# Four graph-attention layers on sixteen graphs: adjacency of two graphs cast on the way into SBUF, weight preparation in the scheduled list, rank tables for the first and last graphs

## The chip, the cores and the metric

The kernel runs on one core of a Trainium2 chip. A core has TensorE (PE, matrix products), VectorE (DVE), ScalarE (ACT), GpSimd (POOL) and SyncE (SP, which issues transfers), each with its own queue of instructions, executed in order. The metric is the device time of one execution in microseconds (us). A measurement of this kernel is the median of several executions.

## The reference

There are B = 16 graphs with N = 1024 nodes and D = 128 features. The input `adj` is [16, 1024, 1024] in int32, each entry 0 or 1, with ones on the diagonal and about one entry in 256 set besides. Four attention layers follow one another, each added to its input and normalised:

```python
x = _layernorm(x + _L0_gnn_ref(x, adj, ...), axis=-1)   # scores by edge type, types 0 and 1 here
x = _layernorm(x + _L1_gnn_ref(x, adj, ...), axis=-1)   # one head, masked by adj > 0
x = _layernorm(x + _L2_gnn_ref(x, adj, ...), axis=-1)   # graph norm, 8 heads, elu, graph norm, 1 head, elu
x = _layernorm(x + _L3_gnn_ref(x, adj, ...), axis=-1)   # one head, masked by adj
```

Layer 0 takes, for each pair of nodes, the score that belongs to its edge type (`take_along_axis` over `src . a_t . dst`), a leaky ReLU, a softmax over all neighbours and a product with the values. Layers 1 and 3 are single-head graph attention: `softmax(where(adj, leaky(s1_i + s2_j), -inf)) @ (x W)`. Layer 2 has an eight-head and a single-head attention of this kind, each behind a normalisation over the graph.

## The kernel before

Nodes are laid out as 128 partitions times G = 8. All data of a graph stay in SBUF from layer to layer. What the attention steps read of the adjacency is `maskT`, the transposed adjacency as fp8 [128, 8, 1024], one per graph, of which four places exist.

**How the order comes about.** `graph(b)` does not issue instructions; it records them. `rc.vector`, `rc.tensor` and the like go to a `Recorder`, which notes each operation, what it depends on and a modelled cost (`cost_of`). `rc.either` notes an operation that two engines can do (a copy, an affine step, the comparison in `products`), and the planner chooses. After all sixteen graphs are recorded, `rc.run(rank, window, later)` plays through the list with the modelled costs: at each step it takes the operation that can start earliest, and among those with equal start the one with the lowest rank. The result is one fixed order for each engine, which `issue` writes out. So nearly all instructions carry one line in the profile, L412, the line in `issue`, and are told apart by the names of their tiles.

The rank of an operation is `graph * STEP + position in its graph + SHIFT[...] + ENDS[graph]`. `SHIFT` has 40 entries over a graph's length, `ENDS` one entry per graph. `later` adds a bias for each engine and kind where an operation may go to two engines. `AHEAD = 3` lets four graphs be open at a time. Tiles come from shelves with a fixed number of places: 28 of `row` (128 x 1032 f32), 8 PSUM banks `bank`, 4 `maskT`, 3 `half`, 2 each of the DRAM scratch `adj` and `up`; a tile's place comes free when its last reader has run. The model prices a cast transfer on POOL at 4 us and 100 bytes per ns.

**Where the mask comes from.** For graph 0 (`b < DIRECT`, `DIRECT = 1`), SyncE loads eight blocks of 128 rows as int32; ScalarE casts each to bf16 and sums it (`e_sum`), TensorE transposes it in eight 128 x 128 pieces, and ScalarE copies the turned block to `maskT` as a square with a second sum (`e_sq`). The two sums, equal when all entries are 0 or 1, are compared at the end. For every other graph, POOL casts the whole adjacency to bf16 in DRAM (`scratch`, profile name `adj`), SyncE issues eight transposing transfers into `half` and eight stores to `upright` (profile name `up`), and POOL brings it back as fp8 into `maskT`. Four ScalarE passes over `maskT` (`half<-maskT`) write a count into `edges`, which is checked at the end. The first cast waits for `begun[0]`, a copy on POOL behind the transposed input `hT` of graph 0.

**Weights.** Some 60 operations ahead of the recorded list, issued directly and therefore first on every queue, load all weights and derive `kwT`, `vpT`, `cbias`, `fold`, `fold_b` (layer 0), `w1_v` (layer 1), `w2a_e`, `w2b_v`, `gn1`, `gn2`, `same_group` (layer 2) and `w3_v` (layer 3). `a_types` is the type tensor of layer 0 turned from [e, t] to [t, e] on POOL. The input of graph 0 is the first load of all, into the place `vs`.

**Layer by layer, per graph.** Layer 0: `transpose_nodes`, three projections, then for two halves of the nodes eight blocks: two products of width 512, `copy_predicated` on `maskT`, a ReLU on ScalarE, a sum with maximum on VectorE, then exponentials and the product with the values. Layers 1, 2b and 3 use `projected_head`: a projection with two score columns, `factors` (a store `a_d` and a load back, broadcast to all partitions), eight masked rows by `weights_of` and 64 products. Layer 2's eight heads use `products`: comparisons on ScalarE or VectorE, a bitwise and with `maskT`, fp8 by bf16 products, and `combine`. The last step is the store to `out` on SyncE. After all graphs a short check over the collected ranges decides whether a general path is run.

Of the kernel before, what the change touches and what calls it, by code (L numbers as in the profile page):

```python
# [109 lines left out]
class Op:  # L110
    __slots__ = ("ways", "way", "skip", "graph", "rank", "before", "after", "ready", "slots", "missing", "late", "kind")


class Recorder:
# [5 lines left out]
    CAST_RATE = 100.0  # L120

    def __init__(self, nc, tc):
        self.nc, self.tc, self.ops, self.graph = nc, tc, [], 0
        self.access = {}

# [36 lines left out]
    def cost_of(self, engine, name, args, kw, outs, ins):  # L162
# [19 lines left out]
        if engine == "gpsimd":  # L182
            if name == "dma_start":
                size = mybir.dt.size(aps[1].dtype) * aps[0].shape[0] * self.width(o)
                return 1500.0, 4000.0 + size / self.CAST_RATE
            return 200.0 + 2.0 * n, 100.0
# [32 lines left out]
    def either(self, *ways, skip=None, kind=0):  # L219
# [6 lines left out]
        op.rank = at = len(self.ops)  # L226
        touched = []
# [37 lines left out]
    def run(self, rank, window, later):  # L265
# [60 lines left out]
        moved = 0.0  # L326

        def admit(i):
            for way in ops[i].ways:
                pools[way[0]].append((i, way, ranks[i] + (later[way[0]][ops[i].kind] if len(ops[i].ways) > 1 else 0)))  # L330
# [25 lines left out]
        while len(order) < n:  # L356
# [41 lines left out]
            if way[0] == "sync":  # L398
                moved = max(moved, end) + way[5]
                op.late = moved - end + self.DMA_FIXED  # L400
            finish(i, end, op.late)
# [22 lines left out]
def gnn_stack_kernel(ctx: ExitStack, tc: tile.TileContext, w: dict, out: bass.AP):  # L424
# [11 lines left out]
    def fast_path(stack):  # L436
# [31 lines left out]
        class Scratch:  # L468


            def __init__(self, *flats):
                self.free, self.named = [(f, 0) for f in flats], {}

            def tile(self, shape, dt, tag, name):
                n = 1
                for v in shape[1:]:
                    n *= v
                if tag not in self.named:
                    k = next(k for k, (f, at) in enumerate(self.free) if at + n <= f.shape[1])
                    f, at = self.free[k]  # L480
                    self.free[k], self.named[tag] = (f, at + n), f[:, at : at + n]
                flat = self.named[tag][0 : shape[0], 0:n]
                if len(shape) > 2:
                    flat = flat.rearrange("p (a b) -> p a b", a=shape[1])
                return flat

        ppool = Scratch(shelves["m4"].places[0], shelves["x4"].places[0])
        turns = [0]

        def ps_const(*shape):  # L490
            turns[0] += 1
            flat = shelves["bank"].places[4 + turns[0] % 4]
            n = 1
            for v in shape:
                n *= v
            return flat[:, 0:n]

        first_x = shelves["vs"].places[0][:, 0 : G * (D + 1)].rearrange("p (g f) -> p g f", g=G)
        nc.sync.dma_start(out=first_x[:, :, 0:D], in_=x_in[0].rearrange("(p g) f -> p g f", g=G))


# [9 lines left out]
        def load(ap, name, shape=(P, D), pool=None):  # L511
            t = (pool or cpool).tile(list(shape), F32, tag=name, name=name)
            nc.sync.dma_start(out=t, in_=ap)
            return t

        def load_rows(vec, n, name):
            return load(vec.partition_broadcast(P), name, (P, n), ppool)

        def column(vec):
            return vec.rearrange("(p o) -> p o", o=1)  # L520

        def transposed(src, name, pool=None):
            ps = ps_const(P)
            nc.tensor.transpose(ps, src, ident)
            t = (pool or cpool).tile([P, P], F32, tag=name, name=name)
            nc.vector.tensor_copy(t, ps)
            return t


        qw = load(w["L0_gnn_qw"], "qw", pool=ppool)  # L530
        kw = load(w["L0_gnn_kw"], "kw", pool=ppool)
        kwT = transposed(kw, "kwT")
        pw = load(w["L0_gnn_pw"], "pw", pool=ppool)
        pwT = transposed(pw, "pwT", ppool)
        vw = load(w["L0_gnn_vw"], "vw", pool=ppool)
        qb = load(column(w["L0_gnn_qb"]), "qb", (P, 1))
        kb = load(column(w["L0_gnn_kb"]), "kb", (P, 1))
        vb = load(column(w["L0_gnn_vb"]), "vb", (P, 1))
        pb = load_rows(w["L0_gnn_pb"], D, "pb")
        ps = ps_const(D)  # L540
        nc.tensor.matmul(ps, lhsT=vw, rhs=pwT, start=True, stop=True)
        vpT = const([P, D], "vpT")
        nc.vector.tensor_copy(vpT, ps)
        vb_wide = ppool.tile([P, P], F32, tag="vb_wide", name="vb_wide")
        nc.vector.tensor_copy(vb_wide, vb.to_broadcast([P, P]))
        ps = ps_const(D)
        nc.tensor.matmul(ps, lhsT=vb_wide, rhs=pwT, start=True, stop=True)
        cbias = const([P, D], "cbias")
        nc.vector.tensor_add(cbias, ps, pb)
        a_types = ppool.tile([P, T, D], F32, tag="a_types", name="a_types")  # L550
        a_raw = ppool.tile([P, D, T], F32, tag="a_raw", name="a_raw")
        nc.sync.dma_start(out=a_raw, in_=w["L0_gnn_a"])
        nc.gpsimd.tensor_copy(a_types, a_raw.rearrange("p e t -> p t e"))


        fold = const([P, 2, D], "fold")
        fold_b = const([P, 2], "fold_b")
        for t in range(2):
            ps = ps_const(D)
            nc.tensor.matmul(ps, lhsT=qw, rhs=a_types[:, t, :], start=True, stop=True)  # L560
            nc.vector.tensor_scalar(fold[:, t, :], ps, 0.2, None, ALU.mult)
            ps = ps_const(1)
            nc.tensor.matmul(ps, lhsT=a_types[:, t, :], rhs=qb, start=True, stop=True)
            nc.vector.tensor_scalar(fold_b[:, t : t + 1], ps, 0.2, None, ALU.mult)

        def score_vector(wt, a_rows, groups, name):
            k = D // groups
            prod = ppool.tile([P, groups, k], F32, tag="prod", name="prod")
            nc.vector.tensor_tensor(
                prod,  # L570
                wt.rearrange("p (g k) -> p g k", g=groups),
                a_rows.unsqueeze(1).to_broadcast([P, groups, k]),
                ALU.mult,
            )
            v = const([P, groups], name)
            nc.vector.tensor_reduce(v, prod, AX.X, ALU.add)
            return v

        def score_weights(wt, a_src, a_dst, groups, name):
            k = D // groups  # L580
            src = score_vector(wt, load_rows(a_src, k, name + "_as"), groups, name + "_src")
            dst = score_vector(wt, load_rows(a_dst, k, name + "_ad"), groups, name + "_dst")
            return src, dst

        def halves(a):
            flat = a if len(a.shape) == 1 else a.rearrange("k o -> (k o)")
            n = flat.shape[0] // 2
            return flat[0:n], flat[n : 2 * n]

        w1 = load(w["L1_gnn_W"], "w1", pool=ppool)  # L590
        w1_s = score_weights(w1, *halves(w["L1_gnn_a"]), 1, "l1")
        w2a = load(w["L2_gnn_W1"], "w2a", pool=ppool)
        w2a_s = score_weights(w2a, *halves(w["L2_gnn_a1"]), NH, "l2a")
        w2b = load(w["L2_gnn_W2"], "w2b", pool=ppool)
        w2b_s = score_weights(w2b, *halves(w["L2_gnn_a2"]), 1, "l2b")
        w3T = transposed(load(w["L3_gnn_W"], "w3", pool=ppool), "w3T", ppool)
        w3_s = score_weights(w3T, *halves(w["L3_gnn_a"]), 1, "l3")


        gn1 = [load(column(w[f"L2_gnn_gn1_{k}"]), f"gn1_{k}", (P, 1)) for k in ("alpha", "scale", "shift")]  # L600

        NA = P // G
        member = ppool.tile([NA, P], F32, tag="member", name="member")
# [9 lines left out]
        gn2_raw = ppool.tile([NA, 3, NH], F32, tag="gn2_raw", name="gn2_raw")  # L613
        for i, k in enumerate(("alpha", "scale", "shift")):
            nc.sync.dma_start(
                out=gn2_raw[:, i, :], in_=w[f"L2_gnn_gn2_{k}"].rearrange("(h a) -> a h", a=NA)
            )
        ps = ps_const(3 * NH)
        nc.tensor.matmul(
            ps, lhsT=member, rhs=gn2_raw.rearrange("a i h -> a (i h)"), start=True, stop=True  # L620
        )
        gn2 = const([P, 3, NH], "gn2")
        nc.vector.tensor_copy(gn2.rearrange("p i h -> p (i h)"), ps)
        ps = ps_const(P)
        nc.tensor.matmul(ps, lhsT=member, rhs=member, start=True, stop=True)
# [559 lines left out]
        for b in range(B):  # L1185
            rc.graph = b
            graph(b)
# [664 lines left out]
```

## Time and profile before

| | |
|---|---|
| time, median of 3 executions | 2499.18 us (2498.39 to 2500.36) |
| profiled execution, its own time | 2502.76 us |
| its span, first to last instruction | 2500.9 us |
| granted TensorE clock, mean | 0.975 |
| busy: PE / PE weight loads | 2351.2 us (94%) / 1999.5 us (80%) |
| busy: VectorE / ScalarE / POOL | 2267.2 us (91%) / 1807.6 us (72%) / 25.1 us (1%) |
| chain that ended last, by engine | PE 58%, DVE 36%, ACT 3%, issue 2%, DMA 1% |
| cast transfers `adj<-in_adj_dram` | 15, 17.6 us from issue to landing (median) |
| return transfers `maskT<-up` | 15, 8.2 us from issue to landing (median) |

The profile is of one execution, so sums of its rows belong to that execution's time, not to the median. An engine's busy share is an average over the whole span, and the stretches of the span have different limits; times within the span count from its first instruction. In a row of instructions "x" is a count, "mean" the duration of one, and "idle before" the time in which the engine had nothing to do just ahead of them, with what ended that wait. An f32 product appears as two records.

### The profile page before, as it was taken

The numbers are of one execution on the slowest core, as the hardware profiler recorded it, in microseconds if no ns is written. First come the engines' busy times: TensorE is split into PE (matmuls) and PEld (weight loads), VectorE is DVE, ScalarE is ACT, GpSimd is POOL, SyncE is SP. The second block draws the span as 40 slices with busy tenths as digits, with TensorE's granted clock in tenths as the row PEclk, the third lists the DMA queues.
The fourth block names the chain that finished last, engine by engine and source line by source line (L and its number), as shares of the span: only waits on it lengthen the run. The fifth ranks groups of instructions, "written<-read, shape, count | busy, mean of one in ns | idle before, by whom it ended". The sixth has DMA issues, their size and how long they took to land.

```text
span 2500.9 us, 56272 instructions
## 1 busy us (share of the span) xinstructions
PE 2351.2 (94%) x22981; PEld 1999.5 (80%) x22981; DVE 2267.2 (91%) x5079; ACT 1807.6 (72%) x3373; POOL 25.1 (1%) x41
## 2 busy tenths in 40 slices
PE   7889999999999999999999999999999999978975
PEld 4758797978979787897869889797888878777965
DVE  3489899999999999999989999999999989889975
ACT  4388595958779686877949688696867858796922
POOL 0000000000000000000000000000000000000000
PEclk8999999999999999999999999999999999989987
DMA  9772226062441706234052442607152222111100
GB/s 223 144 183 49 77 53 174 13 144 86 92 130 21 192 28 139 91 90 132 19 135 86 96 125 50 180 10 171 59 129 93 65 64 86 33 54 48 57 18 27
DMA packets 227738, 229.31 MB, mean 92 GB/s; under 512 B 135056, under 2 KB 171152, under 8 KB 225552
## 3 DMA queue, kind: packets, MB, share of 16 engines
q1 hardware_dynamic: 209712, 178.45, 25.1%
q0 software_dynamic: 17760, 47.19, 10.2%
q8 instruction: 182, 2.98, 0.5%
q14 instruction: 84, 0.69, 0.1%
HBM read 200.76 MB, written 72.02 MB: 109 GB/s over the span
## 4 chain that ended last, share of the span: by engine, by line
PE 58%; DVE 36%; ACT 3%; issue 2%; DMA 1%; POOL 0%; SPq 0%; ACTq 0%; DVEq 0%
PE bank L412 58%; DVE row L412 25%; DVE x L412 5%; ACT row L412 2%; DVE sums L412 1%; DVE bank L412 1%; DVE mv L412 1%; DVE mf L412 1%; DVE m L412 0%; DVE top_all L412 0%; DVE rdens L412 0%; DVE rs_q L412 0%; DVE rden_h L412 0%; DMA m<-in_L_gnn_a_dram 0%; DVE c L412 0%
## 5 line engine op out<-in xcount | busy, mean ns | idle before, releaser
L412 PE MATMUL bank<-row,row 128*128 128x129 f32 (+1 forms) x9216 | 1438.7, 314 | 33.4 <-DVE row L412 19.5
L412 PEld LDWEIGHTS bank<-row,row 128*128 128x128 f32 x9216 | 1122.0, 193 | 215.4 <-issue 143.9
L412 ACT ACTIVATE row<-row,bs2h 128x1024 fp8e4<-128x1024 f32 x684 | 737.7, 1143 | 13.6 <-PE bank L412 13.5
L412 DVE SCALAR_TENSOR_TENSOR row<-row,ratio,maskT 128x1024 f32<-128x1024 f32 x384 | 466.8, 1277 | 12.5 <-DMA row<-a_d 11.5
L412 PEld LDWEIGHTS <-row 128*128 128x128 fp8e4 x8192 | 402.1, 97 | 39.8 <-issue 19.8
L412 PE MATMUL bank<-m,row 128*128 128x102 bf16 x8192 | 420.4, 208 | 10.6 <-DVE row L412 6.2
L412 DVE TENSOR_TENSOR row<-row,maskT 128x2048 uint16<-128x2048 uint16 x256 | 308.9, 1214 | 0.9 <-ACT row L412 0.7
L412 DVE TENSOR_SCALAR row<-row,ns 128x1024 fp8e4<-128x1024 f32 x340 | 244.6, 743 | 0.0
L412 ACT ACTIVATE row<-bank 128x512 f32<-128x512 f32 x256 | 149.4, 594 | 126.1 <-DVE bank L412 114.0
L412 PEld LDWEIGHTS <-maskT 128*128 128x128 fp8e4 x3072 | 201.0, 97 | 24.2 <-issue 22.2
L412 PE MATMUL bank<-m,maskT 128*128 128x136 bf16 x3072 | 211.3, 225 | 5.1 <-DVE m L412 2.6
L412 DVE COPY_PREDICATED bank<-maskT,bank 128x512 f32<-128x512 uint8 x256 | 175.2, 689 | 24.4 <-PE bank L412 23.0
L412 DVE CUSTOM_DVE_ANT_0 row<-bank,row 128x512 f32<-128x512 f32 x256 | 172.8, 681 | 9.9 <-ACT row L412 9.0
L412 PE MATMUL bank<-ident,row 128*128 128x128 f32 x624 | 115.7, 288 | 32.0 <-ACT row L412 24.0
L412 DVE TENSOR_REDUCE x<-bank 128x136 f32<-128x408 f32 x256 | 142.4, 571 | 2.2 <-PE bank L412 1.8
L412 ACT ACTIVATE row<-row,top_all 128x1024 f32<-128x1024 f32 x128 | 139.8, 1141 | 4.9 <-DVE top_all L412 4.8
L412 ACT ACTIVATE row<-row 128x1024 f32<-128x1024 f32 x32 | 33.8, 1056 | 145.1 <-DVE row L412 138.0
L412 ACT ACTIVATE sq<-row 128x128 f32<-128x128 f32 x256 | 76.5, 300 | 84.9 <-DVE row L412 78.9
L412 PEld LDWEIGHTS bank<-ident,row 128*128 128x128 f32 x624 | 78.0, 145 | 58.0 <-ACT row L412 41.9
L412 ACT ACTIVATE half<-maskT,minus_half 128x2048 fp8e4<-128x2048 fp8e4 x60 | 119.6, 1999 | 0.0
L412 DVE SCALAR_TENSOR_TENSOR row<-bank,rdens,row 128x128 f32<-128x128 f32 x368 | 109.6, 342 | 0.2
L412 ACT ACTIVATE row<-bank,exps 128x128 f32<-128x128 f32 x219 | 67.2, 362 | 30.8 <-DVE row L412 29.3
(233 smaller groups left out, 2200.6 us busy)
## 6 DMA issues: line engine op xcount, KB each, us to landing
row<-s1d SPq DMA_DIRECT2D x128, 512.0 KB
adj<-in_adj_dram POOLq DMA_DIRECT2D x15, 2048.0 KB, 17.6
up<-half SPq DMA_DIRECT2D x120, 256.0 KB
row<-a_d SPq DMA_DIRECT2D x48, 512.0 KB
maskT<-up POOLq DMA_DIRECT2D x15, 1024.0 KB, 8.2
out_dram<-row SPq DMA_DIRECT2D x16, 512.0 KB
row<-in_x_dram SPq DMA_DIRECT2D x15, 512.0 KB
row<-in_adj_dram SPq DMA_DIRECT2D x8, 512.0 KB
```

Source lines behind the costliest of these rows:

```text
L412: done = getattr(getattr(self.nc, engine), name)(*[real(a) for a in args], **{k: real(a) for k, a in kw.items()})
```

## The change

Four things change in `fast_path` and in the `Recorder`.

1. `DIRECT` is 2. For graphs 0 and 1 POOL issues four transfers each that cast a quarter of the adjacency from int32 in DRAM to bf16 in SBUF, into `row` places. TensorE transposes each block as before, and the copy into `maskT` is an operation that ScalarE or VectorE can do. `e_sum` and `e_sq` go; the count into `edges` is now made for graphs 0 and 1 too. These casts wait for `begun[0]`, which is now a copy on POOL behind `types`; the casts of the other graphs to DRAM wait for `begun[1]`, the former signal behind `hT` of graph 0. The loads of `x` for graphs 2 and later wait for it as well.
2. The weight preparation is recorded in the list. Layer 0's weights (`weights_of_layer0`, nine loads) come ahead of graph 0 with rank -2000, behind the load of graph 0's input; of the type tensor only two types are turned, on VectorE. All other weights (`weights_of_the_rest`, eighteen loads) are recorded behind layer 0 of graph 0 and ranked at that position.
3. The planner's price of a cast transfer becomes 1 us of issue, 210 bytes per ns one after another, and 4 us at the end.
4. An operation's position `op.at` is counted per graph, with the extra operations of graphs 0 and 1 held at one position. `STEP`, `SHIFT`, `ENDS` and `LATER` have new values, and there are new tables: `FIRST` (20 entries over a graph's length, added for graphs 0 to 2), `FINAL` (20 entries, added for the last three graphs) and `LAST` (added to the engines' biases for the last three graphs).

The diff, cut to its core:

```diff
-    CAST_RATE = 100.0
+    CAST_RATE, CAST_FIXED = 210.0, 4000.0
...
-                return 1500.0, 4000.0 + size / self.CAST_RATE
+                return 1000.0, size / self.CAST_RATE
...
+        op.at = self.counter[self.graph] if self.fixed is None else self.fixed
+        self.counter[self.graph] += self.fixed is None
...
+            if way[1] == "dma_start" and way[0] == "gpsimd":
+                cast = max(cast, end) + way[5]
+                op.late = cast - end + self.CAST_FIXED
...
-        DIRECT = 1
-        e_sum = const([P, DIRECT, G], "e_sum")
-        e_sq = const([P, DIRECT, G], "e_sq")
+        DIRECT = 2
...
+        def weights_of_layer0():
+            pack = row(8, P)
+            kw, qw, vw, pw, pb, pwT, vb_wide = (pack[:, k, :] for k in range(7))
+            a_raw = row(D, T)
+            fetch(kw, w["L0_gnn_kw"])
+            fetch(qw, w["L0_gnn_qw"])
+            fetch(a_raw, w["L0_gnn_a"])
...
+            turned_weight(kwT, kw)
+            types = row(2, D)
+            rc.vector.tensor_copy(types, a_raw.rearrange("p e t -> p t e")[:, 0:2, :])
+            begun.append(rc.gpsimd.tensor_copy(small("begun", P, 1), types[:, 1, D - 1 : D]))
...
+        def weights_of_the_rest():
...
+            value_weights(w1_v, fetch(pack[:, 0, :], w["L1_gnn_W"]), w["L1_gnn_a"], True)
+            value_weights(w2a_e, fetch(pack[:, 1, :], w["L2_gnn_W1"]), w["L2_gnn_a1"], False, NH)
+            value_weights(w2b_v, fetch(pack[:, 2, :], w["L2_gnn_W2"]), w["L2_gnn_a2"], False)
+            w3T = pack[:, 4, :]
+            turned_weight(w3T, fetch(pack[:, 3, :], w["L3_gnn_W"]))
+            value_weights(w3_v, w3T, w["L3_gnn_a"], True)
...
             if b < DIRECT:
-                for ib in range(G):
-                    raw = row(N, dt=I32)
-                    rc.sync.dma_start(out=raw, in_=adj_b[ib])
-                    eb = tile_on("half", [P, N], BF16)
-                    rc.scalar.activation(eb, raw, AF.Identity, accum_out=e_sum[:, b, ib : ib + 1])
-                    ps = bank(G, P, dt=BF16)
-                    for j in range(G):
-                        rc.tensor.transpose(ps[:, j, :], eb.rearrange("p (q g) -> p g q", g=G)[:, j, :], ident_bf)
-                    rc.scalar.activation(
-                        maskT[:, :, ib * P : (ib + 1) * P], ps, AF.Square, saturate=False,
-                        accum_out=e_sq[:, b, ib : ib + 1],
-                    )
+                rc.fixed = rc.counter[b]
+                for k in range(0, G, 2):
+                    eb = row(2, N, dt=BF16)
+                    cast = rc.gpsimd.dma_start(out=eb, in_=adj[b].rearrange("(p g) m -> p g m", g=G)[:, k : k + 2, :])
+                    cast.before[begun[0].rank] = 1
+                    for i in range(2):
+                        ps = bank(G, P, dt=BF16)
+                        for j in range(G):
+                            rc.tensor.transpose(ps[:, j, :], eb[:, i, :].rearrange("p (q g) -> p g q", g=G)[:, j, :], ident_bf)
+                        dst = maskT[:, :, (k + i) * P : (k + i + 1) * P]
+                        rc.either(
+                            ("scalar", "activation", (dst, ps, AF.Copy), dict(saturate=False)),
+                            ("vector", "tensor_copy", (dst, ps), dict(saturate=False)),
+                            kind=1,
+                        )
...
-                cast.before[begun[0].rank] = 1
+                cast.before[begun[1].rank] = 1
...
+            if b == 0:
+                rc.fixed = rc.counter[0]
+                weights_of_the_rest()
+                rc.fixed = None
...
-        AHEAD, STEP = 3, 803
-        LATER = {"vector": (4292, 367, 774), "scalar": (14967, -285, -8493)}
+        AHEAD, STEP = 3, 976
+        LATER = {"vector": (4414, 431, 460), "scalar": (4551, -765, -2672)}
...
+            r = op.graph * STEP + op.at + SHIFT[at * len(SHIFT) // length] + ENDS[op.graph * len(ENDS) // B]
+            if op.graph < 3:
+                r += FIRST[at * n // length]
+            if op.graph >= B - 3:
+                r += FINAL[at * n // length]
+            return r
+
+        def later(op, engine):
+            k = 3 * (engine == "scalar") + op.kind
+            return LATER[engine][op.kind] + (LAST[k] if op.graph >= B - 3 else 0)
```

## The prediction

> **What bounds the kernel now.** I read the page's slices first, to see whether the edges differ from the middle, since the change names the first and the last graphs.
>
> ```profile
> ## 2 busy tenths in 40 slices
> PE   7889999999999999999999999999999999978975
> DVE  3489899999999999999989999999999989889975
> ACT  4388595958779686877949688696867858796922
> ```
>
> A slice is 62.5 us. Between the edges TensorE and VectorE are both near nine tenths in nearly every slice; only the first three and the last five show room. The busy times by stretch give sizes (columns: length, then PE, PEld, DVE, ACT, POOL busy us, granted clock, DMA share, GB/s).
>
> ```profile
> 0.00:10.00 10.00, 2.73 (x10) 1.96 (x10) 1.49 (x20) 1.87 (x2) 1.35 (x9) 1.00 0.57 156
> 10.00:20.00 10.00, 6.14 (x18) 4.12 (x19) 6.83 (x30) 0.69 (x1) 2.49 (x3) 1.00 0.67 165
> 30.00:42.00 12.00, 4.81 (x38) 3.89 (x39) 0.00 (x0) 11.75 (x23) 0.00 (x0) 0.61 1.12 224
> 42.00:100.00 58.00, 58.00 (x291) 38.97 (x290) 34.90 (x103) 29.12 (x54) 0.87 (x1) 0.96 0.74 147
> 100.00:150.00 50.00, 35.07 (x188) 26.55 (x186) 29.57 (x72) 18.37 (x44) 1.11 (x2) 0.83 0.75 159
> 150.00:300.00 150.00, 140.04 (x1341) 114.91 (x1340) 137.81 (x307) 109.18 (x174) 1.41 (x2) 0.99 0.35 84
> ...
> 2200.00:2300.00 100.00, 86.22 (x1119) 82.82 (x1117) 95.30 (x191) 75.89 (x140) 0.00 (x0) 0.91 0.04 12
> 2300.00:2400.00 100.00, 78.78 (x1025) 75.62 (x1023) 95.92 (x194) 75.18 (x124) 0.00 (x0) 0.90 0.18 60
> 2400.00:2501.00 101.00, 61.14 (x443) 58.33 (x443) 60.50 (x145) 24.04 (x90) 0.00 (x0) 0.78 0.09 27
> ```
>
> Three longer stretches (300 to 1000, to 1700, to 2200) have PE at 686.6, 689.4 and 492.6 us: 31.4 us idle of 1900, or 1.65%, with DVE at 94.9%. So the middle is at TensorE's own pace, and what can be won lies at the ends. TensorE is idle 43.5 us of the first 300 (300 less 256.5) and 74.9 us of the last 301.
>
> Next, who waits at the start. From 30 to 42 VectorE does nothing and ScalarE is full: it casts graph 0's adjacency to bf16 (8 times 1.047 + 0.192 us) and copies the turned blocks out of PSUM (8 times 1.02 + 0.19 us). VectorE's first masked copy starts at 46.1. From 100 to 150 TensorE starves because graph 1's mask is late. The order on POOL (start, length) and VectorE's longest wait of the first 200 us show it:
>
> ```profile
> 19.52 0.19 POOL L412 COPY begun<-row 128x1 f32<-128x1 f32 x1 [7.16 <-DVE row L412]
> 19.65 1.90 POOL L412 DMA_DIRECT2D adj<-in_adj_dram  x2
> 106.38 0.57 POOL L412 DMA_DIRECT2D maskT<-up  x1 [33.44 <-DMA up<-half]
> 130.87 0.55 POOL L412 DMA_DIRECT2D maskT<-up  x1 [23.92 <-DMA up<-half]
> ```
>
> ```profile
> DVE row L412 <- PE bank L412: 22.1, 3, 21.1
> ```
>
> The cast of graph 1 is issued at 19.6, but after eight turned transfers and eight stores its mask is asked for only at 106.4 and is there about 8.2 us later, at 115. In between SyncE's queue stood from 68.7 to 99.8 behind graph 0's `a_d` store, with transposes queued behind it. At the end the output stores show that the last graph finishes alone:
>
> ```profile
> 2460.64 0.57 SPq L412 DMA_DIRECT2D out_dram<-row  x1
> 2492.78 0.54 SPq L412 DMA_DIRECT2D out_dram<-row  x1
> ```
>
> **The change, step by step.** Sums go against the profiled execution's 2502.76 us, 3.58 above the median of 2499.18; I subtract that at the end.
>
> *Graph 0's mask.* Before, its eight loads stood behind 28 others in SyncE's queue (15.4 us). Now POOL casts in the transfer, in four pieces of 1 MB read. They wait for a copy behind `types`. Its source `a_raw` was issued at 5.58 and used at 10.36, 4.8 us later; now it is fourth in the queue, issued near 2.7 (the old fourth load's time), so I put the copy at 8 us, against 19.5 for the old signal. A cast of the four times larger piece landed after 14.8 us at best, 17.6 in the middle, 32.7 at worst (the two early ones, beside 5.5 MB of other loads, took 20.6 and 32.7). Per quarter that is 3.7 to 8.2 us. The first half of the mask needs two quarters: 8 + 1.9 (two issues) + 7.4 to 16.4, then some 2 us of turning and copying (1.09 + 1.02), or 20 to 29 us. I take 24, since the competing 4 MB of int32 loads are gone. That is 22 us earlier than 46.1, but only idle time turns into gain. TensorE's idle from 10 to 42 is 11.4 us (3.9 + 0.3 + 7.2). I take 4 of it as left; between 0.5 (the middle's rate) and all 11.4.
>
> *Graph 1's mask.* The cast to DRAM, eight transposes, eight stores and the return transfer go; four casts on POOL follow graph 0's directly. At 3.7 to 8.2 us each, its mask stands at 40 to 75 us, not 115. Its scoring can then fill 100 to 150, where 14.9 us are idle: I take 2 left (0.8 to 14.9). SyncE loses 16 issues there and graph 2's chain moves up by one place, so of the 10 idle us from 150 to 300 I take 5 left (2.5 to 10). Saved at the start: 7.4 + 12.9 + 5.0 = 25.3 us (none to 32.5).
>
> *What is added.* TensorE gets 64 more transposes for graph 1. The old ones took 1.09 us for eight at a clock of 0.61, so 8.7 us; matmuls of 136 bf16 columns come at 67 ns in the middle (142.3 us for 2112), so 4.3. The clock should be higher with graph 0's scoring beside them: 4.3. ScalarE loses graph 0's casts and accumulator reads (9.9 + 1.6 us) and gains the edge count for graph 0 (4 times 2.2 us) and graph 1's eight copies (8.2): 5.5 more, costed at nothing, as ScalarE is idle 51 us of the first 100; without that cover 5.5. Sixteen copies may also go to VectorE, at most twice its 683 ns for 512 columns, 22 us, below its idle 75 us of the first 150. Net start: 25.3 - 4.3 = **21 us saved** (8.7 lost to 28 saved).
>
> *Weights.* Layer 0's keep their nine small loads ahead. The rest (18 loads at 0.45, 8 us of SyncE, and about 30 small VectorE operations at 0.15 to 0.3, 7 us) move into the list behind layer 0. SyncE has nothing urgent then: it stood 31 us behind `a_d`. VectorE is idle 23 of the 58 us from 42 to 100. I put it at nothing; with the cover gone, 7 us, and graph 0's layer 1 is next late, which queues on TensorE behind `w1_v`. The expanding copy on POOL (2.01 us) becomes a VectorE copy of two types; inside the 8 us above. Of the three VectorE steps dropped from the final check only one stood at the end (0.14 us): nothing.
>
> *POOL's queue.* All eight casts precede graph 2's. If a cast waited for a free `row` buffer, graph 2's transfers would be late; they are wanted only once graph 0 and 1 have been scored, after 100 us. No cost.
>
> The Trainium skill's "SBUF — State Buffer", section "SBUF: two separate sides", speaks against putting eight more transfers on POOL: while VectorE runs an operation that takes both port pairs, POOL cannot write descriptors, so its transfer waits. The row here is POOL's 15 cast issues, 866 to 1027 ns each, most of them beside a VectorE that is over 90% busy, which shows no such blocking. By the page's own pair of figures (620 ns alone, 3100 beside such a copy) the eight casts would take about 20 us longer in all and graph 0's half 5 us, and the sum, as an estimate, would keep some 14 of the 21 us.
>
> *The last graphs.* Tables for the last three graphs move operations in order and between ScalarE and VectorE. From 2200 to 2400 VectorE is full (191 of 200) and ScalarE has 49 us free; from 2400 on a chain of single graphs leaves both half empty. VectorE's 251.7 us of work at the middle's 94.9% would take 265, so 36 of 301 us is the most that order alone can give; a badly fitted table can also lose, and I bound that at 10, a third of the 32 us between the last two stores. Two heads ending together can't hide the last statistics and stores. I take somewhat under half: **16 us**.
>
> *The middle.* The step, all 40 shifts and the engine biases are replaced too. One point of TensorE's idle share there is 19 us. The profile cannot say which way; at 1.65% there is little to win. I take 0, and half a point, 10 us, each way for the range.
>
> Sum: 2502.8 - 21 - 16 = 2465.8, less 3.6 is **2462 us**.
>
> **The rivals.** (A) Both ends give nearly all that the stretches allow: start 28, end 30, middle 6: 2435 us. For it: the idle time is real and each cause is addressed; against it: the last graph's chain still has to drain. (B) Only the start gains: 17 us, the end's order no better: 2482. For it: the late part is a chain of dependent steps (`a_d` store and load alone 5.6 us at 2463.6). (C) The change does nothing measurable: the earlier masks are hidden since TensorE is already full from 42 to 100, and the later idle time moves to graph 2, whose mask comes the old way: 2499. (D) Slower: the new table orders the middle worse, so that TensorE runs dry between graphs. The gains of 37 us are used up once the idle share of the middle exceeds 1.65 + 37/19 = 3.6%; at 4.5% it is 2462 + 54 = 2516. For it: the old table reaches 98.4%, so almost any other can only lose; against it: four graphs may be open at once, so there is other work to pick.
>
> **How the numbers follow.** My forecast (2445 to 2472) gets 0.42, A 0.20, B 0.22, C 0.04, D 0.12. Faster by over 0.2% (about what a measurement can tell from no change) are the forecast, A and B: 0.84; within it C: 0.04; slower D: 0.12. The range runs from 2430, just under A, to 2502, past C, and leaves out the worse half of D and the extreme of A.
>
> **What would show it.** Right: VectorE's first masked copy at 20 to 29 us; graph 1's last block of the mask before 75; TensorE's idle in the first 300 us near 18 to 24 instead of 43.5; ScalarE's share up and PE idle near 55 to 60 in the last stretch; last two output stores closer than 32 us; the middle's idle near 1.6%. Wrong: casts landing later than 8 us apiece, weights' steps ahead of graph 0's scores on VectorE, a gap of TensorE at graph 2's mask, or a middle whose TensorE share moves by more than a point: that alone would outweigh either end.

## The result and the profile after

The changed kernel takes 2508.41 us (median of 20 runs, 2505.30 to 2511.32) where the kernel before takes 2503.84 us beside it (20 runs, 2497.77 to 2509.77): a ratio of 1.0022, 95% interval 1.0014 to 1.0029. It is slower by 0.2%: the interval lies clear of 1, though the two sets of runs overlap. The forecast was 2462 us. The profiled execution after took 2508.62 us with a span of 2506.5 us.

The page's slices of the changed kernel (62.5 us each, in tenths):

```profile
PE   5999999999999999999999999999999899998975
DVE  2589899999999999999999999999999899999985
ACT  2678594968869596886959688694776859787842
```

The first slice has become emptier (TensorE 5 for 7, ScalarE 2 for 4), the second and third are fuller on TensorE. The busy times by stretch of the changed kernel, with the columns of the prediction (length, then PE, PEld, DVE, ACT, POOL busy us, granted clock, DMA share, GB/s), say how much:

```profile
0.00:10.00 10.00, 5.53 (x14) 3.45 (x15) 2.34 (x20) 2.62 (x4) 3.25 (x14) 1.00 0.59 158
10.00:20.00 10.00, 4.99 (x21) 2.63 (x19) 2.73 (x16) 3.22 (x6) 3.07 (x6) 0.87 0.96 158
20.00:30.00 10.00, 5.03 (x18) 4.00 (x19) 2.25 (x10) 0.69 (x1) 0.72 (x2) 0.50 1.08 202
30.00:42.00 12.00, 0.57 (x3) 0.28 (x2) 2.42 (x8) 0.00 (x0) 0.70 (x1) 0.64 1.12 212
42.00:100.00 58.00, 47.73 (x225) 28.00 (x226) 23.02 (x59) 27.95 (x36) 0.54 (x1) 0.86 0.89 179
100.00:150.00 50.00, 48.44 (x295) 34.81 (x294) 39.23 (x85) 35.22 (x52) 1.42 (x2) 1.00 0.38 92
150.00:300.00 150.00, 143.62 (x1335) 116.09 (x1334) 136.31 (x322) 108.10 (x193) 0.00 (x0) 0.99 0.21 60
300.00:1000.00 700.00, 683.51 (x6961) 589.50 (x6960) 672.35 (x1501) 531.62 (x933) 7.25 (x10) 1.00 0.39 97
1000.00:1700.00 700.00, 688.02 (x6877) 588.09 (x6876) 672.12 (x1547) 553.54 (x1001) 6.23 (x8) 1.00 0.38 95
1700.00:2200.00 500.00, 480.71 (x4452) 398.14 (x4449) 461.80 (x1060) 356.30 (x647) 3.43 (x5) 0.99 0.33 89
```

From 100 to 150 TensorE has 48.4 us where it had 35.1, but not only as meant: graph 0, whose sixteenth and last masked copy starts at 98.7 instead of 72.0, now reaches into this stretch, and graph 1's first masked copy starts at 124.6, only 9 us earlier than before (133.8). From 42 to 100 TensorE has 47.7 where it had 58.0, and from 30 to 42 almost nothing. TensorE's idle time (length less PE busy), summed, is a ledger of the whole difference:

| us | 0–300 | 300–1700 | 1700–2200 | 2200–end | PE busy | span |
|---|---|---|---|---|---|---|
| before | 43.5 | 24.0 | 7.4 | 74.8 | 2351.2 | 2500.9 |
| after | 44.1 | 28.5 | 19.3 | 62.2 | 2352.4 | 2506.5 |
| change | +0.6 | +4.5 | +11.9 | −12.6 | +1.2 | +5.6 |

The end gained 12.6 us, the start nothing, and the middle lost 16.4. The waits of the first 100 us of the changed kernel (total, times, longest) name what took the gain at the start:

```profile
PE bank L418 <- DMA gn_raw<-in_L_gnn_gn_shift_dram: 14.9, 1, 14.9
POOL row L418 <- DMA adj<-in_adj_dram: 13.9, 1, 13.9
PE bank L418 <- DMA row<-in_L_gnn_W_dram: 10.0, 1, 10.0
ACT half L418 <- DMA up<-half: 9.6, 1, 9.6
```

And its timeline (start, length, engine, operation, count, idle before and its releaser) puts them in order:

```profile
8.22 1.02 POOL L418 DMA_DIRECT2D adj<-in_adj_dram  x1
9.36 3.72 POOL L418 DMA_DIRECT2D row<-in_adj_dram  x7
24.95 0.33 SPq L418 DMA_DIRECT2D gn_raw<-in_L_gnn_gn_shift_dram  x1
24.98 0.47 PE L418 MATMUL bank<-ident,row 128*128 128x128 f32 x1 [9.98 <-DMA row<-in_L_gnn_W_dram]
45.48 0.58 PE L418 MATMUL bank<-gn_raw,member 16*128 16x24 f32 x2 [14.90 <-DMA gn_raw<-in_L_gnn_gn_shift_dram]
45.99 6.45 PE L418 MATMUL bank<-row,row 128*128 128x512 f32 x8
57.22 0.70 DVE L418 COPY_PREDICATED bank<-maskT,bank 128x512 f32<-128x512 uint8 x1 [10.94 <-ACT maskT L418]
73.38 2.00 ACT L418 ACTIVATE half<-maskT,minus_half 128x2048 fp8e4<-128x2048 fp8e4 x1 [9.58 <-DMA up<-half]
```

Graph 0's score products (the eight matmuls at 45.99) stand on TensorE directly behind a product of 16 by 24 with the second graph norm's three vectors, weights of a later layer. That one waits 14.9 us for the last of them, the shift, a load of half a kilobyte in single values of 4 bytes, which SyncE issued at 24.95 and which came 20 us later, beside the casts (DMA share 1.08 to 1.12). The first masked copy follows at 57.2; before it stood at 46.1. The transposes of graph 0's mask stand behind the same product, and ScalarE's edge count for graph 0 starts only at 73.4, behind a transfer of graph 2.

### The profile page after: what moved, and what is told of

Read it like the earlier page. It is cut to its first block, busy times and chain, and to the rows that moved or that the text cites. A ratio compares the mean times of both kernels' runs of the same rounds, so it can differ in the third digit from the quotient of the medians.

```text
span 2506.5 us, 56383 instructions
## 1 busy us (share of the span) xinstructions
PE 2352.4 (94%) x23045; PEld 2000.9 (80%) x23045; DVE 2278.5 (91%) x5201; ACT 1816.1 (72%) x3233; POOL 26.6 (1%) x47
## 4 chain that ended last, share of the span: by engine, by line
PE 54%; DVE 35%; ACT 6%; issue 2%; DMA 2%; SPq 1%; ACTq 0%; DVEq 0%
PE bank L418 54%; DVE row L418 24%; ACT row L418 5%; DVE x L418 4%; DVE bank L418 2%; SPq L418 1%; DVE mv L418 1%; DVE sums L418 1%; DMA row<-in_L_gnn_a_dram 1%; DVE m L418 1%; DVE mf L418 1%; DMA half<-adj 0%; DVE rdens L418 0%; DMA up<-half 0%; DVE top_all L418 0%
## 5 line engine op out<-in xcount | busy, mean ns | idle before, releaser
L418 PE MATMUL bank<-row,row 128*128 128x129 f32 (+2 forms) x9220 | 1441.6, 314 | 39.8 <-DVE row L418 21.9
L418 ACT ACTIVATE row<-row,bs2h 128x1024 fp8e4<-128x1024 f32 x773 | 830.6, 1141 | 4.8 <-DVE row L418 4.8
L418 DVE SCALAR_TENSOR_TENSOR row<-row,ratio,maskT 128x1024 f32<-128x1024 f32 x384 | 469.9, 1274 | 12.6 <-PE bank L418 9.3
L418 PEld LDWEIGHTS <-row 128*128 128x128 fp8e4 (+1 forms) x8320 | 415.9, 99 | 62.7 <-issue 34.2
L418 PE MATMUL bank<-m,row 128*128 128x102 bf16 x8192 | 430.6, 209 | 21.2 <-DVE row L418 14.1
L418 DVE TENSOR_SCALAR row<-row,ns 128x1024 fp8e4<-128x1024 f32 x251 | 182.9, 744 | 0.0
L418 ACT ACTIVATE half<-maskT,minus_half 128x2048 fp8e4<-128x2048 fp8e4 x64 | 127.4, 1994 | 9.7 <-DMA up<-half 9.6
L418 PE MATMUL bank<-ident,row 128*128 128x128 f32 x643 | 107.4, 286 | 28.1 <-DVE row L418 14.6
L418 DVE SCALAR_TENSOR_TENSOR row<-bank,rdens,row 128x128 f32<-128x128 f32 x384 | 115.3, 341 | 0.5
## 6 DMA issues: line engine op xcount, KB each, us to landing
row<-in_adj_dram POOLq DMA_DIRECT2D x8, 512.0 KB, 25.1
```

The source lines that it names most:

```text
L418: done = getattr(getattr(self.nc, engine), name)(*[real(a) for a in args], **{k: real(a) for k, a in kw.items()})
```

## The experiments

Two theories. The first: the weight steps, moved into the list, hold up graph 0, because every engine takes its operations in order and a step that waits for a late load holds all behind it. The second: the quarter casts themselves are late, or the new tables cost what the start gives. In all kernels below but those with other tables, the planner decides as in the changed kernel, and only the named operations are moved in the finished order, or given another place, before it is issued.

**Small loads first, graph 2's cast last, and both.** After the planner's order is made, listed operations are taken out and put right behind an anchor:

```
# e1: layer 3's weight and six graph norm loads go behind layer 0's loads
+ rc.moves.append((fetches[18:19] + fetches[21:27], fetches[8]))
# e2: graph 2's cast goes behind the eight quarter casts
+ rc.moves.append((casts[8:9], casts[7]))
# e3: both lines
```

> Only SyncE's order differs from the changed kernel: the load of layer 3's weights and the six small loads of the graph norms stand right behind layer 0's loads instead of last. Theory 1 (TensorE's in-order queue: two weight products of later layers stand ahead of graph 0's scores and wait for these loads, 10.0 and 14.9 us): both waits shrink to under 3 us, VectorE's first masked copy comes at 35 to 45 us instead of 57.2, and the time falls by 10 to 20 us, to about 2490. Theory 2 (the transfers' bandwidth: the 2 MB cast of graph 2 and eight quarter casts land late in any order): TensorE then waits for the quarter casts instead, the first masked copy stays after 50 us, and the time stays within 4 us of 2508.

> Only POOL's order differs from the changed kernel: graph 2's cast to DRAM is issued behind the eight quarter casts of graphs 0 and 1 instead of ahead of them. Theory 2 (bandwidth): the quarter casts land some 15 us sooner, the first masked copy comes at about 40 us, and the time falls by about 10 us. Theory 1 (small loads on TensorE's queue): the wait for the graph norm's loads stays near 15 us, as they still stand behind the casts on the DMA engines, the first masked copy stays within 5 us of 57, and the time stays within 4 us of 2508.

> Both moves of order together. Theory 1: as with the small loads alone, plus a few us; first masked copy at 25 to 35 us, the time at 2483 to 2492. Theory 2: as with the cast moved alone, 2498, the small loads adding nothing. If neither moves the time by 4 us although the first masked copy comes 20 us sooner, the early start is hidden, which was the prediction's rival C.

Measured: 2507.12 us, ratio to the kernel before 1.0018 (1.0008 to 1.0027); 2506.15, 1.0015 (1.0005 to 1.0024); 2508.39, 1.0023 (1.0014 to 1.0033). None moves the time by more than 3 us from the changed kernel, and the first masked copy came at 53.2, 57.3 and 52.6 us. The named waits do go, and others take their place. The waits of e2 in the first 100 us show one of the two moved from one operand to the next:

```profile
PE bank L441 <- DMA row<-in_L_gnn_W_dram: 18.2, 1, 18.2
PE bank L441 <- DMA gn_raw<-in_L_gnn_gn_shift_dram: 9.0, 1, 9.0
```

The timeline of e3 shows what is late when neither load is:

```profile
23.24 0.28 DVE L441 TENSOR_REDUCE mean<-row 128x1 f32<-128x128 f32 x1 [12.67 <-DMA row<-in_L_gnn_W_dram]
23.78 5.49 PE L441 MATMUL bank<-row,fold 128*128 128x512 f32 x6 [12.20 <-DVE fold_b L441]
73.71 2.00 ACT L441 ACTIVATE half<-maskT,minus_half 128x2048 fp8e4<-128x2048 fp8e4 x1 [14.52 <-DMA up<-half]
```

VectorE waits for a weight and TensorE for VectorE: the weight steps hold two engines, not one queue. And the edge count started at 71.8 to 73.7 us in all three, in e3 after 14.5 us of waiting. My first theory in the form "these small loads are late" does not hold: with them moved ahead, another weight's load is the late one. What e1 to e3 leave is the steps themselves, and ScalarE's count.

**The count in a place of its own.** The four counts of graph 0 write a scrap copy of the mask, of which only the sum is used, to one of three places called `half`, through which the turned transfers of graph 2 also pass. In e5 they write to a place that is idle at that time:

```
  count = tile_on("half", [P, G // 4, N], F8)
+ if b == 0:
+     rc.own.append((count.tile, shelves["vs"]))
```

This run was made after e6 and e7 below, and its expectation leans on them; theory 3 is that ScalarE's queue is held at this count.

> The changed kernel with one alteration: graph 0's four counts write into the idle place vs instead of a `half` place; the weights' steps and graph 2's cast stay where they are. Theory 3 with theory 1 (two holds in a row, the weights' steps on TensorE and VectorE, then the count on ScalarE, and what one gives back the other takes): here only the second goes, ScalarE's wait of 9.6 us for `up<-half` disappears, the first masked copy stays near 57 us, and the time falls by 6 to 12 us, to 2496 to 2502. If the count's wait alone explained the late start, the time would fall to 2482, as with all three moves.

Measured: 2501.06 us, ratio 0.9991 (0.9982 to 1.0000). So 7.3 us of the changed kernel hung on one scrap place. The first masked copy stays at 57.5, and TensorE still waits 16.5 us for the graph norm's shift: that hold-up is untouched.

**The weight steps behind graph 0's mask.** In e6 graph 2's cast goes last, and every weight step of the later layers that isn't a load (but `same_group`, which needs none) is placed behind graph 0's eighth masked copy, with scratch places of its own so that nothing else is moved by it:

```
+ rc.own += [(pack.tile, shelves["m4"]), (vectors.tile, shelves["x4"])]
+ rc.behind = ([op for op in rc.ops[start:] if op.ways[0][0] != "sync"], preds[7])
+ rc.moves.append((casts[8:9], casts[7]))
```

> The planned order of the changed kernel with two moves: graph 2's cast behind the eight quarter casts, and all steps of the later layers' weights other than their loads moved, on TensorE, VectorE and ScalarE, from ahead of graph 0's scores to behind its eighth masked copy (their scratch lies in the idle places m4 and x4, their product in a PSUM bank that is free there). Theory 1 (these steps hold up the in-order queues): the first masked copy comes at 24 to 35 us instead of 52.6. Theory 3 (ScalarE's queue is held at graph 0's count, which waits for one of the three `half` places that graph 2's transposed transfers occupy): ScalarE's wait for the store `up<-half` grows from 14.5 to 25 to 40 us, it ends near 74 us as in all runs so far, and the time stays within 4 us of 2508. Rival to theory 3: the wait does not bind, and the time falls by 15 us or more.

Measured: 2516.02 us, ratio 1.0047 (1.0033 to 1.0061). The first masked copy is at 25.4 us, where the prediction had put it, and the time is worse. Its masked copies, its first 300 us and the waits of the first 100 say why:

```profile
L462 DVE COPY_PREDICATED bank<-maskT,bank x33: 674/692/697, 25.4 to 196.7; 128x512 f32<-128x512 uint8 x33
0.00:300.00 300.00, 244.00 (x1850) 179.54 (x1850) 202.46 (x505) 176.74 (x285) 9.82 (x24) 0.93 0.45 102
ACT half L462 <- DMA up<-half: 39.9, 1, 39.9
PE bank L462 <- DVE top L462: 36.4, 2, 35.5
```

The count waits 39.9 us for the place `half`; VectorE's `top` and then TensorE wait behind it. It starts at 71.9, where it always did. Hence the next.

**All three together, and without the cast.** e7 is e6 with the counts in the place `vs`; e11 is e7 without the moved cast.

> As with the weights' steps moved, and graph 0's four counts write into the idle place vs instead of a `half` place. Theory 3: ScalarE's wait for `up<-half` is gone, TensorE's idle time of the first 100 us falls from 36 to under 22, and the time falls by 12 to 20 us, to 2488 to 2496. Rival C of the prediction (an early start is hidden because a later wait, at graph 2's mask near 150 us, takes it): TensorE's idle time falls before 100 us and rises by as much between 100 and 300, and the time stays within 4 us of 2508.

> The version with all three moves without the move of graph 2's cast, which goes back ahead of the eight quarter casts. If the transfers' order on POOL matters once nothing else holds up the start, the first masked copy comes at 34 to 40 us instead of 24.8 and the time is 2488 to 2496; if the masks were early enough anyway, it is within 3 us of 2482.

Measured for e7: 2481.86 us, ratio 0.9915 (0.9901 to 0.9928), the fastest version with e12 below, 26.6 us under the changed kernel and so more than the 12 to 20 expected. For e11: 2486.35 us, ratio 0.9944 (0.9923 to 0.9965), first masked copy at 36.0; the mask came as the first of the two theories said, the time rose less than it said. The masked copies of e7 (durations, first and last start in the first 200 us), and ScalarE's first count in its timeline, now without a wait:

```profile
L462 DVE COPY_PREDICATED bank<-maskT,bank x34: 665/694/697, 24.8 to 198.2; 128x512 f32<-128x512 uint8 x34
```

```profile
31.25 2.03 ACT L462 ACTIVATE vs<-maskT,minus_half 128x2048 fp8e4<-128x2048 fp8e4 x1
```

The stretches of e7:

```profile
0.00:300.00 300.00, 275.91 (x2224) 211.59 (x2225) 235.05 (x569) 202.17 (x317) 9.96 (x24) 0.98 0.51 117
300.00:1000.00 700.00, 683.64 (x6740) 579.57 (x6738) 669.48 (x1534) 527.57 (x964) 7.39 (x10) 1.00 0.39 97
1000.00:1700.00 700.00, 687.97 (x6974) 590.73 (x6973) 672.85 (x1504) 542.07 (x958) 7.49 (x10) 1.00 0.39 98
1700.00:2200.00 500.00, 480.90 (x4571) 405.63 (x4570) 460.80 (x1071) 370.79 (x657) 1.97 (x3) 0.99 0.29 81
```

TensorE idles 24.1 us of the first 300 instead of 44.1; the other stretches are those of the changed kernel to within 0.5 us (19.1 idle from 1700 to 2200, 61.8 from 2200 on). Of the 26.6 us, 20.0 are that idle time, 5.9 are less busy time of TensorE (2346.5 for 2352.4, at a granted clock of 0.983 for 0.978 over the span), and 0.7 the rest. Beside each other:

| first masked copy, idle of PE 0–300, time (us) | counts in `half` | counts in `vs` |
|---|---|---|
| weight steps where planned | 57.2, 44.1, 2508.4 | 57.5, 41.8, 2501.1 |
| weight steps behind the mask, cast 2 last | 25.4, 56.0, 2516.0 | 24.8, 24.1, 2481.9 |
| the same, cast 2 not moved | not run | 36.0, 27.6, 2486.4 |

The two gains don't add: 7.3 us alone, a loss of 7.6 alone, 26.5 together. Each hold-up hid the other. The order of the casts is worth 4.5 us by these medians once both are gone, 7 by the ratios (0.9944 and 0.9915), whose intervals just overlap; e12 below, which has e7's order of the casts and was measured beside e11, is 5.0 us faster than e11.

**More of the same.** e12 is e7 with the small loads of e1 first and the weight steps behind the 16th masked copy (`preds[15]`).

> The version with all three moves, with two more: layer 3's weights and the six small loads stand behind layer 0's loads, and the weights' steps stand behind graph 0's sixteenth masked copy instead of the eighth. If TensorE's wait of 4.1 us at 43 to 48 us (for the turned weight of layer 3) binds, the time falls by 2 to 5 us, to 2477 to 2480; if it is hidden, it stays within 2 us of 2482.

Measured: 2481.31 us, ratio 0.9920 (0.9902 to 0.9937), the same as e7. TensorE idles 23.0 us of the first 300, 1.1 less than in e7, and nothing of it shows in the time.

**The tables.** Four kernels ask what the tables of the changed kernel are worth. e4 sets those of the last graphs to zero (`FINAL = (0,) * 20`, `LAST = (0,) * 6`); e8 gives the changed kernel the tables, step and length of the one before; e9 gives the kernel before the new ones; e10 is e7 with `FINAL` zero.

> The tables FINAL and LAST are all zero, so the last three graphs are ranked as the middle ones are; all else is the changed kernel's. If those tables are worth what was predicted, the time rises by 10 to 20 us. If they give at the end (TensorE idle 12.6 us less after 2200) what they take between 1700 and 2200 (11.9 us more), the dip near 1950 us goes and the time stays within 5 us of 2508.

> The changed kernel with the rank tables and biases of before (step 803, the old shifts over the old length, no tables for first and last graphs); casts, weights in the list and planner costs are the new ones. If the new tables lose in the middle what they gain at the end (TensorE idle: 16.4 us more from 300 to 2200, 12.6 less after), the middle goes back to about 31 us of idle time and the end to about 75, and the time is 2500 to 2510. If the new tables are what makes the new list work at all, the time rises by more than 20 us.

> The kernel before with the new step, shifts, biases and tables for first and last graphs, and nothing else of the change. If the tables' effect is the one read from the two traces, TensorE's idle time is about 48 us in the middle and 62 after 2200, with the old start, and the time is 2500 to 2515. If the tables fit only the list that they were made for, the middle or the end loses much more and the time is above 2525.

> The version with all three moves, with the table FINAL alone set to zero; LAST and the rest stay. If FINAL buys its gain at the end with the idle time between 1700 and 2200, TensorE's 19.1 us there fall to 9 to 12, the end's 62 rise to about 75, and the time is within 6 us of 2482. If the dip has nothing to do with FINAL, the 19 us stay and the time rises by what FINAL is worth at the end, 10 to 30 us.

Measured: e4 2634.02 us, ratio 1.0524 (1.0508 to 1.0540); e8 2633.18, 1.0517 (1.0503 to 1.0532); e9 3005.36, 1.1998 (1.1982 to 1.2015); e10 2525.07, 1.0099 (1.0080 to 1.0117). e4 misses what either theory gave by far. e8 and e9 came out as the second theory of each had it, and so don't tell structure from tables as they were meant to. e10, 43.2 us over e7, is above what both of its theories gave. The slices of TensorE in e9:

```profile
PE   7795999769999599479996956969897949879775
```

Idle time is spread over the whole span. With the last graphs' tables zeroed (e4), or all swapped either way (e8, e9), 125 to 500 us are lost: the tables fit the list of operations they stand with. So the change can't be split into "structure" and "tables" in this manner, and what each would give with the other fitted to it stays open.

e10 stays near enough to be read, with care: its profiled execution, 2518.30 us, is the fastest of its four. The stretch of it that answers to 480.90 above:

```profile
1700.00:2200.00 500.00, 475.08 (x4438) 397.02 (x4439) 450.72 (x1043) 362.18 (x652) 1.97 (x3) 0.99 0.29 80
```

From 1700 to 2200 it idles 24.9 us, more than the 19.1 with `FINAL`, and from 2200 to its span of 2516.3 us 84.8 instead of 61.8; another 8.8 us are busy time of TensorE (2355.3 for 2346.5). So in this list `FINAL` is worth some 23 us of idle time at the end, and taking it out does not give the stretch before it its time back. What `LAST` does was not tried by itself.

**The middle.** That stretch had, before,

```profile
1700.00:2200.00 500.00, 492.60 (x4614) 412.02 (x4614) 464.04 (x1053) 371.40 (x698) 3.42 (x5) 1.00 0.34 91
```

and after it has 480.7 to 481.2 us of TensorE in the changed kernel, e1, e2, e3, e5, e6, e7 and e11, though the idle time of their first 300 us runs from 24.1 to 56.0 (e12 has 478.6). It therefore belongs to the planned order and not to anything that the start hands on. In the changed kernel 12.3 of the 19.3 us lie between 1925 and 2050:

```profile
1925.00:2050.00 125.00, 112.70 (x1256) 101.64 (x1256) 111.91 (x231) 87.43 (x138) 0.00 (x0) 0.99 0.28 78
```

The kernel before has 123.4 us of TensorE in those 125. VectorE is idle there too (13 us), one wait of it on TensorE of 8.3 us and otherwise waits of 1 to 4 us in both directions. Whether it comes of the tables, of the new prices or of the longer list stays open: none of them can be set back without all later decisions changing.

## Why the prediction was wrong, point by point

**Graph 0's mask (forecast 24 us, in 20 to 29; after, 57.2).** The working of the casts held: with what stood in the way taken out (e6, e7) the first masked copy is at 25.4 and 24.8. The step that failed is the one headed "Weights", which I put at nothing ("with the cover gone, 7 us"). I looked for the cover in VectorE's idle time and SyncE's queue, that is, at how long the steps take. Their price is where they stand: they are ahead of graph 0's scores on TensorE and VectorE and wait for loads that come late beside the casts. The prediction lists "weights' steps ahead of graph 0's scores on VectorE" among the signs of being wrong, yet gave it no price. On TensorE's queue, where the two longest waits stand, it looked only at graph 0's layer 1 behind `w1_v`. Standing behind the mask instead, the same steps cost 12 to 15 us less once the count is out of the way too (e11 against e5, by ratios and by medians).

**ScalarE's edge count ("costed at nothing, as ScalarE is idle 51 us of the first 100").** Also failed, by 7.3 us alone and by 34.2 in e6 (2516.0 to 2481.9). Its time is indeed free; its output place wasn't. Only with both steps mended is most of the start's gain there: the idle time of the first 300 us is 24.1 in e7, a tenth above the 18 to 24 that I gave, 20.0 below the changed kernel's and 19.4 below that of the kernel before, where 25.3 were forecast.

**"POOL's queue. All eight casts precede graph 2's … No cost."** False in its premise: the signal for graph 2's cast fired first, it was issued at 8.22, and the quarter casts behind it took 25.1 us in the middle (first line) instead of 15.3 in e2 (second):

```profile
row<-in_adj_dram POOLq DMA_DIRECT2D x8, 512.0 KB, 25.1
row<-in_adj_dram POOLq DMA_DIRECT2D x8, 512.0 KB, 15.3
```

With the other hold-ups there it cost nothing that shows in the time (e2), with them gone 4.5 us (e11 against e7).

**Graph 1's mask (12.9 us forecast).** TensorE's idle time from 100 to 150 us did go, from 14.9 to 1.6, but the sign for it, graph 1's last mask block before 75 us, was missed, at 111.2 after and at 78.5 in e7. In the changed kernel graph 0's late work reaches into the stretch, so there the number is in part luck. In e7 the casts themselves were early: all eight quarters had landed by 35.7 us, and TensorE, busy with graph 0, turned graph 1's blocks only from 65.6 on, where its order has them. My reading of the old stretch was half right: graph 1's mask was there at 116, and 7.2 of the 14.9 idle us lie at 128 to 135, where TensorE waits for ScalarE behind graph 0's layer 1.

The blocking of POOL beside VectorE, which the prediction had cited, is not seen, but hardly tested either: the quarter casts' issues took 533 to 581 ns each, seven of the eight at 9.4 to 13.1 us, and VectorE was busy only 2.7 of the 10 us from 10 to 20. (The 14 of the 21 us that the prediction would keep with it are not worked out there.) What looks crowded is the transfers themselves, with a DMA share of 1.08 to 1.12 while SyncE's half kilobyte took 20 us; how much of that is the crowd and how much its single values was not tried. The Trainium skill's "DMA: Bandwidth & Descriptors", section "Issuing engines are not separate DMA queues", says that transfers of different engines interleave on the same 16 DMA engines, and this case agrees with it. Its section "Latency and other measured facts" gives a tiny transfer a floor of about 0.8 us, 25 times less than measured here under that load.

**The last graphs (16 forecast, 12.6 measured).** Right in sign and near in size: idle time from 2200 on fell from 74.8 to 62.2, and the sign I gave (55 to 60 us idle in the last stretch) was not reached. In e10's list `FINAL` alone is worth more than all of it. The last two stores, however, moved apart, not together:

```profile
2445.54 0.57 SPq L418 DMA_DIRECT2D out_dram<-row  x1
2498.51 0.54 SPq L418 DMA_DIRECT2D out_dram<-row  x1
```

They are 53 us apart against 32, so that sign was wrong. The gain lies ahead of them, in the first two of these stretches:

```profile
2200.00:2300.00 100.00, 95.87 (x1253) 93.21 (x1251) 97.58 (x213) 90.13 (x138) 0.00 (x0) 0.98 0.07 25
2300.00:2400.00 100.00, 85.67 (x1161) 83.00 (x1160) 97.55 (x202) 81.85 (x135) 0.00 (x0) 0.93 0.18 60
2400.00:2507.00 107.00, 62.75 (x460) 59.70 (x458) 68.84 (x166) 24.87 (x91) 0.00 (x0) 0.79 0.08 26
```

There TensorE has 181.5 us in place of 165.0, and ScalarE 172.0 in place of 151.1: ScalarE took over work beside a VectorE that was full, as the prediction had read the place. From 2400 to the end TensorE idles 4 us more than before (43.8 for 39.8).

**The middle (0, within 10 either way; measured −16.4).** This term was mis-sized, outside its own bounds, and its cause stays open. The idle share from 300 to 2200 went from 1.65 to 2.5% (47.8 of 1900), below the 3.6% from which rival D said that a better start and end would be used up. D's mechanism is part of what happened, but it decided only because the start gave nothing: with the start of e7 the same middle leaves a gain of 22 us.

**The sum.** Forecast 21 + 16 + 0; measured in idle time −0.6 + 12.6 − 16.4, less 1.2 of TensorE's work, which is −5.6. The 21 hold 4.3 of added work; with the 1.2 counted there, about 23 us of the miss lie at the start, 16 in the middle, 3 at the end. Of the 4 left over, 3.6 are what I took off to come from the profiled execution (2502.76) to the median of three (2499.18): in 20 runs the kernel before took 2503.84, so there was nothing to take off. By its time rival D came nearest (2516 at an idle share of 4.5%); rival C (2499) had a start that gives nothing, but for a reason that wasn't so: TensorE full from 42 to 100. No rival priced steps that stand ahead of graph 0.

## What to carry to other kernels

A step that is moved costs what stands behind it while it waits, not how long it takes: before putting one at nothing, look at each engine's order around its new place, at the load that it waits for and at the place that it writes to. When a mended wait leaves the time where it was, look for the next one at the same spot, and mend them together before giving up the theory: here one mend won 7.3 us alone, the other lost 7.6, and together they won 26.5. A table of due times fits one list of operations, and even a well-fitted change of it should be read stretch by stretch: here an end that gained 12.6 us stood behind a stretch that lost 11.9.

## What the runs showed of the hardware

A load of 0.5 KB, in single values of 4 bytes, took 20 us from issue to landing while the casting transfers were under way, and SyncE's issues then began 1.4 to 3.9 us apart, where one itself takes 0.33. POOL issued eight casts in a row, the one that reads 4 MB and seven quarters, and waited 13.9 us with the last quarter until the first had landed. In e7 eight quarters went out in a row, and the ninth cast, graph 2's, was issued at 16.7, just after the first had landed at 16.4. That one goes to DRAM, so what it waits for isn't a place in SBUF; whether the limit of eight is the queue's or that of the signals which the program waits on isn't shown. TensorE's granted clock goes roughly with how busy it is at the start: over the first 100 us it is 0.78 in e6 (52.7 us busy), 0.81 in the changed kernel (63.9) and 0.95 in e7 (82.8). That fits with the 5.9 us of busy time that e7 saves beside its idle time.
